# Graph attention on one Trainium2 core: degree rows, checks, strip loads and the last attention sums at other steps

## The chip, the core and the metric

The kernel runs on one core of a Trainium2 chip. The core has five engines that work side by side and wait for one another through semaphores: TensorE (PE in the profile, with its weight loads as PEld) multiplies matrices into PSUM, VectorE (DVE), ScalarE (ACT) and GpSimd (POOL) work elementwise, and SyncE (SP) issues transfers. The metric is the device time of one execution in microseconds.

## What is computed

A graph of N = 2708 nodes with D = 128 features, a 0/1 matrix `adj` of 2708 x 2708, in two layers. Only the first layer and its end matter here:

```python
def _L0_gnn_ref(t, x, adj, alpha, beta):
    deg = jnp.clip(adj.sum(axis=1), 1.0)
    dis = deg ** (-0.5)
    adj_norm = dis[:, None] * adj * dis[None, :]
    diffusion = adj_norm @ x - x
    norms = jnp.maximum(jnp.linalg.norm(x, axis=-1), COS_EPS)
    sim = x @ x.T / (norms[:, None] * norms[None, :])
    attn = jax.nn.softmax(beta * sim * adj, axis=1)
    return diffusion + jax.nn.sigmoid(alpha) * (attn @ x - x)

x = _layernorm(x + _L0_gnn_ref(L0_gnn_t, x, adj, L0_gnn_alpha, L0_gnn_beta), axis=-1)
x = _layernorm(x + _L1_gnn_ref(x, adj, L1_gnn_W, L1_gnn_a), axis=-1)
```

The second layer (`_L1_gnn_ref`: two products with `adj` around an attention without softmax) takes the time from about 300 us on and isn't touched.

## The kernel before

**Tiles.** The nodes are cut into NB = 22 blocks of 128 rows (the last holds 20) and into strips of SW = 512 columns: strips 0 to 4, and strip 5, the "side" strip, with the remaining 148 columns. Four blocks make a group, groups 0 to 5, the last of two blocks. `adj_t` is the transposed matrix; a "piece" is one group of blocks of one strip, 1024 KB.

**Attention.** The loop `for n, s in enumerate(order)` takes the strips in the order 2, 3, 4, 1, 0, so n = 0 is strip 2 ("the first place") and n = 4 is strip 0 (the last). The side strip is worked on together with n = 3. In each strip 22 steps k run over the blocks `jb` in the order `taken`: 8 to 21, then 4 to 7, then 0 to 3, that is over the groups 2, 3, 4, 5, 1, 0. A step does:

- TensorE makes `sim` (a product of the normalized rows, or, for blocks whose strip was done before, a transpose of a kept copy).
- VectorE multiplies it with beta and the piece into `p_t` (line 212; six buffers, EARLY + 3), ScalarE takes the exponential (line 217), GpSimd adds it to `total` (line 222), and TensorE adds `x_sb` times `p_t` to `att_acc` in PSUM (line 207). In the first strip, TensorE's last product lags three steps.
- When a group is through, its piece of the next strip is loaded into the same room on SP's queue.

Around these steps, work for later is put at fixed steps:

- `degree(ib, h)` loads half a row block of `adj` (677 KB, on SP) into one of three rooms, `row0`, `row1` and the back part of `x1` (blocks 6 and up; its front part is the `total` of n = 3), and ScalarE adds it up. There are 44 half rows; `rows_at[n]` lists the steps at which one is taken from the list `todo`.
- `roots(b0, b1)` turns the sums into `deg`, `live` and `dis` (the power -0.5, on GpSimd). `x_sb` is then scaled with `dis` on VectorE (line 742) after steps 11, 15, 19 and 21 of the last strip, block by block as the attention's products have read it.
- In the last strip, `round_part(g)` copies the pieces of strip 0 into tiles of the diffusion (VectorE, a cast), `check_part(g)` adds up the low 16 bits of a piece on ScalarE, writing its elementwise result into a scratch room, and `load_part(1, g)` loads the piece of strip 1 for the diffusion into the same room, issued on GpSimd's queue. A load needs the check, the rounding and all uses of the old piece.
- `attended(s, acc, total)` ends a strip: TensorE sums `total` over the partitions (`sums`, 8 small matmuls, line 528), VectorE takes reciprocals, ScalarE copies `acc` from PSUM (`to_sbuf`), TensorE turns it (`turned`), VectorE adds it to `att` (line 538). For a strip it stands at step 5 of the next one; for strip 0 it stands behind the loop.

**Diffusion.** After the loop `x_sb` is split into a rounded part and a rest, `x_hi` and `x_lo` (`halves`, line 224). Then `for s in (NS - 1, 0, 1, 2)` takes the strips 5, 0, 1, 2: `diffuse(s, acc)` adds up 22 blocks times two parts in `dif_acc` (the side strip uses `x_sb` itself, in one part), `load_strip(s + 2)` asks for the strip after next, and `summed_up`, `normed`, `x1_turned`, `scores`, `tally` and so on make the first layer's result out of it. `attended` of strip 0 stands behind the products of strip 5, before those of strip 0. Strips 3 and 4 follow in an order written out by hand.

**What sets the order.** Each engine works through its own list in order. `pinned` ties an instruction behind the last pinned one of its engine. In the first strip (`strict` holds an entry) all instructions of the helpers at lines 198 to 222 are pinned, in the order of the program. Later only what stands in `in_order(...)` is pinned, behind the step that it belongs to; all else is ordered by the builder, from its own estimate of when each instruction is ready, the earlier in the program first. Line 198 of the profile is the helper of pinned instructions, lines 207, 212, 217 and 222 those of unpinned ones on TensorE, VectorE, ScalarE and GpSimd.

PSUM: `ps_acc` has two banks for accumulators, `tp` and `tp2` are two banks handed out in turn by `tp_bank` for sums and transposes. SBUF: copies made by `to_sbuf` share two buffers.

Of the kernel before, what the change touches and what calls it, by code (L numbers as in the profile page):

```python
# [12 lines left out]
I16 = mybir.dt.int16  # L13
# [5 lines left out]
P = 128  # L19
N = 2708  # L20
D = 128
NB = (N + P - 1) // P
NP = NB * P
LAST = N - (NB - 1) * P
SW = 512
# [22 lines left out]
def grouped(  # L48
# [46 lines left out]
    x1 = late.tile([P, NB, D], F32, name="x1")  # L95
# [139 lines left out]
    def to_sbuf(acc, v, nb):  # L235

        t = lp.tile([P, SW], F32, tag="to_rows", name="tr_sb", bufs=2)
        if v < nb * P:
            nc.gpsimd.memset(t[:, v : nb * P], 0.0)
        act("copy", t[:, :v], acc[:, :v])  # L240
        return t
# [8 lines left out]
    def turned(t, nb):  # L250

        rows = tp_bank("tr_ps")
        for b in range(nb):
            mm(nc.tensor.transpose, rows[:, b, :], t[:, ts(b, P)], ident)
        return rows
# [38 lines left out]
    groups = list(dict.fromkeys(b // 4 for b in taken))  # L294
# [39 lines left out]
    with ExitStack() as es:  # L334
        pz = pool("pz", EARLY + 3, side="right", stack=es)
        pa = pool("pa", side="right", stack=es)
        row_rooms = [pa.tile([P, N // 2], F32, name=f"row{k}") for k in range(2)]
# [158 lines left out]
        def in_order(f):  # L496

            latest.update(behind)
            strict.append("some")
            f()  # L500
            strict.pop()
# [13 lines left out]
        def roots(b0, b1):  # L515

            t = deg[:, b0:b1]
            dve("tensor_tensor", t, deg2[:, b0:b1, 0], deg2[:, b0:b1, 1], ALU.add)
            dve("tensor_scalar", live[:, b0:b1], t, 0.0, None, ALU.is_gt)
            dve("tensor_scalar", t, t, 1.0, None, ALU.max)  # L520
            gps("tensor_tensor", dis[:, b0:b1], t, minus_half[:, b0:b1], ALU.pow)

        def attended(s, acc, total):

            v, nb = width(s), blocks(s)
            sums = tp_bank("sums")
            for b in range(nb):
                nc.tensor.matmul(
                    sums[:, b, 0:1], total[:, ts(b, P)], ones[:, 0:1], start=True, stop=True
                )  # L530
            rsum = small.tile([P, SW // P], F32, tag="rsum", name="rsum")
            nc.vector.reciprocal(rsum[:, :nb], sums[:, :nb, 0])
            nc.vector.tensor_scalar(rsum[:, :nb], rsum[:, :nb], sig, None, ALU.mult)
            rows = turned(to_sbuf(acc, v, nb), nb)
            for b in range(nb):
                ib = s * 4 + b
                r = att[:, ib, :]
                nc.vector.scalar_tensor_tensor(
                    r, rows[:, b, :], rsum[:, b : b + 1], r, ALU.mult, ALU.add
                )  # L540
# [1 line left out]

        room_of = {2: "room5", 3: "room1", 4: "room3", 1: "room0", 0: "room4", 5: "room2"}
        rounded_at = {2: 5, 3: 8, 4: 12, 1: 15, 0: 18, 5: 19}
        checked_at = {2: 13, 3: 18, 4: 21, 5: 21}
        strips = {0: {}, NS - 1: kept_c}

        def part_of(s, g):
# [10 lines left out]
        def check_part(g, room=None):  # L559
            low_bits_of(  # L560
                kept_a[g].rearrange("p b i -> p (b i)"),
                room or row_rooms[g % 2].bitcast(I16),
            )

        def load_part(s, g):
            src = adj_t[4 * g * P : min(4 * g + 4, NB) * P, ts(s, SW)]
            pinned(
                "strips", gps, "dma_start", part_of(s, g),
                src.rearrange("(b p) i -> p b i", p=P),
            )  # L570
# [6 lines left out]
        ended = []  # L577
        scaled = set()
        for n, s in enumerate(order):
            wide = n == side_n  # L580
            w_all = SW + SHORT if wide else SW
            acc = ps_acc.tile([P, SW], F32, tag="acc", name="att_acc")
            if wide:
                total = x1[:, :6, :].rearrange("p b i -> p (b i)")
# [3 lines left out]
            else:  # L588
                total = lp.tile([P, SW], F32, tag="total", name="total", bufs=2)
# [10 lines left out]
                (1, 17): lambda: constants(2),  # L600
                (2, 11): lambda: roots(0, 8),
                (3, 20): lambda: roots(8, 18),
                (4, 12): lambda: roots(18, NB),
            }

            rows_at = {
                0: (18, 20), 1: range(0, NB, 2), 2: range(0, NB, 2),
                3: [k for k in range(21) if k % 3 < 2], 4: range(0, 12, 2),
            }
            turns = {  # L610
                3: lambda: turn_rows(12, 16, by_dve),
# [20 lines left out]
            for k, jb in enumerate(taken):  # L632
# [91 lines left out]
                if n == len(order) - 1:  # L724
                    for g in [g for g, at in rounded_at.items() if at == k]:
                        in_order(lambda: round_part(g))
                    if k in (17, 20):
                        in_order(lambda: load_part(1, groups[k > 17]))
                    for g in [g for g, at in checked_at.items() if at == k]:
                        in_order(lambda: check_part(g))  # L730
                    if k in (11, 15, 19, 21):

                        done = sorted(taken[: k + 1 if k == NB - 1 else k - 1])
                        done = [b for b in done if b not in scaled]
                        scaled.update(done)
                        while done:
                            b0 = b1 = done[0]
                            while b1 in done:
                                done.remove(b1)
                                b1 += 1  # L740
                            xs = x_sb[:, b0:b1, :]
                            nc.vector.tensor_tensor(
                                xs, xs,
                                dis[:, b0:b1].unsqueeze(2).to_broadcast([P, b1 - b0, D]),
                                ALU.mult,
                            )
# [267 lines left out]
    for s in (NS - 1, 0, 1, 2):  # L1014
        acc = ps_acc.tile([P, SW], F32, tag="acc", name="dif_acc")
        diffuse(s, acc)
        if s < 3:
            load_strip(s + 2)
        if s == NS - 1:
            attended(*ended.pop())  # L1020
            for g in (1, 0):
                check_part(
                    g, work2.tile([P, 2048], I16, tag="low", name="low_junk", bufs=1)
                )
            for g in groups[2:]:
                load_part(1, g)
        if s == 1:
            flat = kept_c.rearrange("p b i -> p (b i)")
            v = SHORT
            for b0, b1 in ((0, NB // 2), (NB // 2, NB)):  # L1030
                low_bits_of(
                    flat[:, b0 * v : b1 * v],
                    work2.tile([P, 2048], I16, tag="low", name="low_junk", bufs=1),
                )
        normed(s, summed_up(s, acc))
        x1_t = x1_in_sbuf(s, x1_turned(s))
        pbs = []
        for k in (1, 0):
            pb = scores(s, x1_t, k, score_bank())
            tally(s, pb, k)  # L1040
            pbs.append(pb)
        shared_row(s, pbs[0])
        picked(s, pbs[0], sr_p)
        picked(s, pbs[1], sc_p)
        limited(s * 4, s * 4 + blocks(s))
        e2(s * 4, s * 4 + blocks(s))
        if s == 1:
            fill("e")
# [577 lines left out]
    k = 0  # L1626
# [568 lines left out]
```

## Time and profile before

| | |
|---|---|
| median of 3 runs | 649.35 us (648.65 to 652.32) |
| the profiled execution | 652.04 us, span 649.3 us |
| PE busy | 608.8 us, 94% |
| DVE busy | 491.4 us, 76% |
| ACT busy | 471.3 us, 73% |
| POOL busy | 289.2 us, 45% |
| first strip of the attention | about 9 to 50 us |
| last strip of the attention | about 174 to 219 us |
| diffusion | from 219.88 us (first product of strip 0) to about 290 us |

The span runs from the first to the last instruction of the profiled execution; its time has some 2.7 us more around it. That execution took 2.69 us more than the median of the runs. Sums of durations below come from this one execution.

Two engines share lines in the profile: where a tile's name ends in a digit the digit is left out, so `x<-` can be `x1`, and `row<-pieces` is a check that writes its scratch into `row0` or `row1`.

### The profile page before, as it was taken

Reading aid. Unit: us, or ns where it says so; the run is one execution under the profiler, and the core shown is the slowest. Engines: PE = TensorE matmul, PEld = TensorE weight load, DVE = VectorE, ACT = ScalarE, POOL = GpSimd, SP = SyncE. Lnnn points to the kernel's source line nnn. Section 1 sums busy time; section 2 is a strip of 40 time slices with the busy share of each in tenths; the row PEclk is TensorE's granted clock in tenths of the full one; section 3 lists DMA queues with packets and bytes.
Section 4 is the critical chain, followed back from the end, with each engine's and each line's share of the span. In section 5 each row is a group of like instructions: output and inputs, shape, how many; then the busy total and the mean of one; then the engine's idle time right before and its main releaser. Section 6 shows DMA issues by size and latency. Waiting matters only on the chain.

```text
span 649.3 us, 8555 instructions
## 1 busy us (share of the span) xinstructions
PE 608.8 (94%) x2859; PEld 351.9 (54%) x2859; DVE 491.4 (76%) x978; ACT 471.3 (73%) x649; POOL 289.2 (45%) x270
## 2 busy tenths in 40 slices
PE   7999999999999899998878899999999999989993
PEld 4445345465655676765664344444444444658872
DVE  5765865764699756756885999899999999599575
ACT  4767786767889521410585999999999999778652
POOL 6967778777798742000123322333232230021573
PEclk9999999999999899999988999999999999999997
DMA  8968989988971999989956999756689453259981
GB/s 270 392 221 330 317 301 363 360 329 310 335 262 70 276 390 389 387 267 375 394 205 185 238 223 246 214 168 175 193 217 267 170 170 129 87 202 383 390 320 53
DMA packets 66407, 171.64 MB, mean 264 GB/s; under 512 B 10059, under 2 KB 19285, under 8 KB 63333
## 3 DMA queue, kind: packets, MB, share of 16 engines
q1 hardware_dynamic: 42500, 107.01, 46.4%
q0 software_dynamic: 22464, 62.25, 34.5%
q10 hardware_dynamic: 1392, 1.77, 0.8%
q8 instruction: 24, 0.39, 0.2%
q14 instruction: 27, 0.21, 0.1%
HBM read 171.89 MB, written 5.72 MB: 274 GB/s over the span
## 4 chain that ended last, share of the span: by engine, by line
PE 65%; ACT 13%; DVE 10%; POOL 6%; issue 4%; DMA 1%; another core or an unknown queue 0%; DVEq 0%; POOLq 0%; ACTq 0%
PE num L198 11%; PE m_acc L198 11%; PE att_acc L207 9%; PE h_acc L1690 7%; PE sim L207 7%; PE dif_acc L207 6%; ACT q L198 5%; POOL total L222 4%; ACT L198 2%; DVE q L198 2%; PE tot L198 2%; PE dif_acc L198 1%; PE sim L198 1%; POOL ss L198 1%; ACT xn L198 1%
## 5 line engine op out<-in xcount | busy, mean ns | idle before, releaser
L198 PE MATMUL m_acc<-q,xws 128*128 128x512 f32 x240 | 121.6, 592 | 0.0
L198 PE MATMUL num<-ring,wt 128*128 128x512 f32 x216 | 98.2, 546 | 3.6 <-DVE q L198 2.2
L222 POOL TENSOR_TENSOR total<-total,p_t 128x512 f32<-128x512 f32 (+1 forms) x67 | 91.8, 1370 | 21.0 <-ACT p_t L217 18.4
L207 PE MATMUL att_acc<-p_t,x_sb 128*128 128x512 f32 x184 | 91.1, 602 | 1.1 <-ACT p_t L217 1.1
L212 DVE SCALAR_TENSOR_TENSOR p_t<-sim,gentle,pieces 128x512 f32<-128x512 f32 x89 | 65.0, 746 | 34.8 <-PE sim L207 25.7
L198 DVE SCALAR_TENSOR_TENSOR q<-sr_b,nc_s,q 128x1536 f32<-128x1536 f32 (+1 forms) x48 | 77.8, 1623 | 17.3 <-ACT q L198 17.3
L217 ACT ACTIVATE p_t<-p_t,shift 128x512 f32<-128x512 f32 (+1 forms) x89 | 64.7, 745 | 33.8 <-DVE p_t L212 31.5
L198 DVE COPY q<-num 128x512 f32<-128x512 f32 (+1 forms) x142 | 83.5, 611 | 4.5 <-PE num L198 4.5
L198 PEld LDWEIGHTS m_acc<-q,xws 128*128 128x128 f32 x240 | 45.3, 190 | 55.0 <-issue 54.8
L198 ACT ACTIVATE q<-q,head,rest 128x1536 f32<-128x1536 f32 (+1 forms) x48 | 70.2, 1508 | 1.6 <-DVE ring L198 1.3
L198 ACT ACT_TABLE_LOAD x52 | 66.7, 1283 | 3.9 <-issue 3.1
L198 PEld LDWEIGHTS num<-ring,wt 128*128 128x128 f32 x216 | 39.0, 190 | 49.1 <-issue 34.2
L198 ACT ACTIVATE q<-q,c_s 128x1536 f32<-128x1536 f32 (+1 forms) x48 | 62.9, 1355 | 0.3
L198 POOL DMA_INDIRECT ring<-in_adj_t,k_no x18 | 20.8, 1154 | 89.1 <-PE num L198 85.6
L207 PEld LDWEIGHTS att_acc<-p_t,x_sb 128*128 128x128 f32 x184 | 31.7, 189 | 35.3 <-ACT p_t L217 18.8
L207 PE MATMUL sim<-xn_t 128*128 128x512 f32 x98 | 47.6, 592 | 0.0
L222 POOL TENSOR_TENSOR x<-x,p_t 128x660 f32<-128x660 f32 (+1 forms) x22 | 35.1, 1596 | 11.3 <-ACT p_t L217 10.6
L198 ACT ACTIVATE row<-row 128x1354 f32<-128x1354 f32 x30 | 39.5, 1318 | 0.3 <-DMA row<-in_adj 0.3
L207 PE MATMUL dif_acc<-strip,x_hi 128*128 128x512 f32 x88 | 37.8, 429 | 0.0
L207 PE MATMUL dif_acc<-strip,x_lo 128*128 128x512 f32 x88 | 36.2, 411 | 0.0
L1690 PE MATMUL h_acc<-rounded,m_hi 128*128 128x512 f32 x88 | 32.4, 407 | 3.7 <-DVE rounded L212 3.7
L198 PE MATMUL num<-x_sb,wt 128*128 128x512 f32 (+1 forms) x72 | 34.4, 570 | 0.7 <-ACT gb L198 0.7
(362 smaller groups left out, 1170.6 us busy)
## 6 DMA issues: line engine op xcount, KB each, us to landing
pieces<-in_adj_t SPq DMA_DIRECT2D x24, 1024.0 KB, 6.8
strip<-in_adj_t POOLq DMA_DIRECT2D x20, 1024.0 KB, 18.3
row<-in_adj SPq DMA_DIRECT2D x30, 677.0 KB, 5.5
nat<-in_adj_t SPq DMA_DIRECT2D x19, 768.0 KB, 7.7
x<-in_adj SPq DMA_DIRECT2D x14, 677.0 KB, 6.2
ring<-in_adj_t SPq DMA_DIRECT2D x9, 1024.0 KB, 5.1
pieces<-in_adj_t SPq DMA_DIRECT2D x7, 512.0 KB, 6.4
x_sb<-in_adj_t SPq DMA_DIRECT2D x4, 768.0 KB, 6.2
```

What stands on the lines that cost most here:

```text
L198: latest[engine] = op(*args, **kwargs)
L207: op(*args, **kwargs)
L212: return getattr(nc.vector, op)(*args, **kwargs)
L217: return getattr(nc.scalar, op)(*args, **kwargs)
L222: return getattr(nc.gpsimd, op)(*args, **kwargs)
L1690: nc.tensor.matmul(acc[:, : rows.shape[-1]], m[:, kb, :], rows, start=(kb, part) == (0, 0), stop=(kb, part) == (NB - 1, 1),)
```

## The change

- `rows_at`: the first strip takes half rows at steps 13, 15, 17, 18 and 20 instead of 18 and 20; the last one at steps 0, 2 and 4 instead of 0, 2, 4, 6, 8 and 10. All half rows in between keep their steps, and each step now takes the row that is three places further in the list.
- `prep`: the last roots stand at step 7 of the last strip instead of 12.
- `checked_at`: checks of groups 2, 3, 4, 5 stand at steps 9, 13, 18, 20 instead of 13, 18, 21, 21, and their scratch room is the back part of `x1` instead of `row0` and `row1`.
- `asked_at`: the loads of strip 1's groups 2 and 3 stand at steps 13 and 16 instead of 17 and 20.
- `attended` of strip 0 is split: the copy out of PSUM (`to_sbuf`) stays behind strip 5's products, and the rest (sums, transposes, VectorE's part) stands behind strip 0's products.

```diff
--- before.py
+++ after.py
@@ -520,7 +520,7 @@
             dve("tensor_scalar", t, t, 1.0, None, ALU.max)
             gps("tensor_tensor", dis[:, b0:b1], t, minus_half[:, b0:b1], ALU.pow)
 
-        def attended(s, acc, total):
+        def attended(s, acc, total, t=None):
 
             v, nb = width(s), blocks(s)
             sums = tp_bank("sums")
@@ -531,7 +531,7 @@
             rsum = small.tile([P, SW // P], F32, tag="rsum", name="rsum")
             nc.vector.reciprocal(rsum[:, :nb], sums[:, :nb, 0])
             nc.vector.tensor_scalar(rsum[:, :nb], rsum[:, :nb], sig, None, ALU.mult)
-            rows = turned(to_sbuf(acc, v, nb), nb)
+            rows = turned(t or to_sbuf(acc, v, nb), nb)
             for b in range(nb):
                 ib = s * 4 + b
                 r = att[:, ib, :]
@@ -542,7 +542,8 @@
 
         room_of = {2: "room5", 3: "room1", 4: "room3", 1: "room0", 0: "room4", 5: "room2"}
         rounded_at = {2: 5, 3: 8, 4: 12, 1: 15, 0: 18, 5: 19}
-        checked_at = {2: 13, 3: 18, 4: 21, 5: 21}
+        checked_at = {2: 9, 3: 13, 4: 18, 5: 20}
+        asked_at = {2: 13, 3: 16}
         strips = {0: {}, NS - 1: kept_c}
 
         def part_of(s, g):
@@ -559,7 +560,7 @@
         def check_part(g, room=None):
             low_bits_of(
                 kept_a[g].rearrange("p b i -> p (b i)"),
-                room or row_rooms[g % 2].bitcast(I16),
+                room or x1[:, 6:, :].rearrange("p b i -> p (b i)").bitcast(I16),
             )
 
         def load_part(s, g):
@@ -600,12 +601,12 @@
                 (1, 17): lambda: constants(2),
                 (2, 11): lambda: roots(0, 8),
                 (3, 20): lambda: roots(8, 18),
-                (4, 12): lambda: roots(18, NB),
+                (4, 7): lambda: roots(18, NB),
             }
 
             rows_at = {
-                0: (18, 20), 1: range(0, NB, 2), 2: range(0, NB, 2),
-                3: [k for k in range(21) if k % 3 < 2], 4: range(0, 12, 2),
+                0: (13, 15, 17, 18, 20), 1: range(0, NB, 2), 2: range(0, NB, 2),
+                3: [k for k in range(21) if k % 3 < 2], 4: (0, 2, 4),
             }
             turns = {
                 3: lambda: turn_rows(12, 16, by_dve),
@@ -724,8 +725,8 @@
                 if n == len(order) - 1:
                     for g in [g for g, at in rounded_at.items() if at == k]:
                         in_order(lambda: round_part(g))
-                    if k in (17, 20):
-                        in_order(lambda: load_part(1, groups[k > 17]))
+                    for g in [g for g, at in asked_at.items() if at == k]:
+                        in_order(lambda: load_part(1, g))
                     for g in [g for g, at in checked_at.items() if at == k]:
                         in_order(lambda: check_part(g))
                     if k in (11, 15, 19, 21):
@@ -1017,13 +1018,15 @@
         if s < 3:
             load_strip(s + 2)
         if s == NS - 1:
-            attended(*ended.pop())
+            in_sbuf = to_sbuf(ended[0][1], SW, SW // P)
             for g in (1, 0):
                 check_part(
                     g, work2.tile([P, 2048], I16, tag="low", name="low_junk", bufs=1)
                 )
             for g in groups[2:]:
                 load_part(1, g)
+        if s == 0:
+            attended(*ended.pop(), in_sbuf)
         if s == 1:
             flat = kept_c.rearrange("p b i -> p (b i)")
             v = SHORT
```

## The prediction

> **What bounds the kernel now.** I read the share of busy time first, then the stretches around the change, then the chain of waits, then each engine in order of time. TensorE is busy 94% of the span, so a change pays only where TensorE stands still, and that is the end of the attention:
>
> ```profile
> 187.00:206.00 19.00, 18.86 (x69) 10.08 (x69) 18.86 (x23) 18.66 (x27) 17.84 (x10) 1.00 0.47 153
> ```
> ```profile
> 206.00:220.00 14.00, 10.14 (x54) 7.25 (x52) 11.10 (x12) 10.14 (x15) 12.59 (x13) 0.98 0.42 115
> ```
>
> The columns are stretch, length, then busy time of PE, PEld, DVE, ACT, POOL, granted clock, DMA share and GB/s. From 187 to 206 four engines are full at once. From 206 to 220 TensorE is idle for 14.00 - 10.14 = 3.86 us: this is what there is to win here. GpSimd is the fullest there. The chain of waits says the same:
>
> ```profile
> 205.55 1.53 issue
> 207.19 0.92 issue
> 208.11 1.27 POOL total L222
> ...
> 217.28 1.29 POOL total L222
> 218.62 1.08 PE sums L528 x8
> ```
>
> The chain runs along GpSimd's additions, stops 1.5 us in front of the roots, and ends in the sums of strip 0. The order of time shows why it stopped (VectorE, then TensorE):
>
> ```profile
> 204.34 1.23 DVE L198 TENSOR_TENSOR deg<-deg 128x4 f32<-128x4 f32 x1
> 205.49 0.74 DVE L212 SCALAR_TENSOR_TENSOR p_t<-sim,gentle,pieces 128x512 f32<-128x512 f32 x1
> 206.15 0.15 DVE L198 TENSOR_SCALAR live<-deg 128x4 f32<-128x4 f32 x1
> 206.22 0.74 DVE L212 SCALAR_TENSOR_TENSOR p_t<-sim,gentle,pieces 128x512 f32<-128x512 f32 x1
> 206.88 0.15 DVE L198 TENSOR_SCALAR deg<-deg 128x4 f32<-128x4 f32 x1
> 208.17 3.43 DVE L742 TENSOR_TENSOR x_sb<-x_sb,dis 128x512 f32<-128x512 f32 x2 [1.14 <-POOL dis L198]
> 213.37 0.69 DVE L742 TENSOR_TENSOR x_sb<-x_sb,dis 128x512 f32<-128x512 f32 x1 [1.76 <-PE att_acc L207]
> 213.97 1.43 DVE L212 CAST x_hi<-x_sb 128x384 fp32r<-128x384 f32 x1
> ```
> ```profile
> 209.98 0.77 PE L207 MATMUL dif_acc<-side,x_sb 128*128 128x148 f32 x4 [1.31 <-DVE x_sb L742]
> 210.59 2.74 PE L207 MATMUL att_acc<-p_t,x_sb 128*128 128x512 f32 x6
> ...
> 218.62 1.08 PE L528 MATMUL sums<-ones,total 128*128 128x1 f32 x8 [2.55 <-POOL total L222]
> ```
>
> One late number goes round all engines. The last half row is added up behind step 10 (ScalarE, done at 200.97). Its degrees reach VectorE at 204.34, the root is ready on GpSimd at 208.13, the scaling of x_sb waits 1.14 for it, TensorE waits 1.31 for the scaling, and the last att_acc products queue behind that. The last scaling waits 1.76 for them, and only then does x_hi start, without which no product of strip 0's diffusion can. Last, TensorE waits 2.55 for the sums.
>
> **The change, part by part.** The yardstick is the first dif_acc product of strip 0, at 219.88 now; from there to 270 TensorE shows no idle time, so a shift there is handed on.
>
> Rows. A half row costs ScalarE 1.31 us (199.66 to 200.97). Three go from the last strip to steps 13, 15 and 17 of the first, 3.9 us each way. In the first strip ScalarE waited 1.43, 1.43 and 0.98 us before the exponentials that follow those steps, so two are covered and the third makes one exponential 0.33 us late; TensorE's products lag three steps there (3 x 1.72 us), which hides that. Their transfers (3 x 677 KB, 2.08 MB) are issued on SP in front of pieces of the next strip, which are not used before 50 us; 40 to 50 moved 178 GB/s against 391 at 20 to 30, so there is room. Cost taken: 0; without the cover 3.9 us (see the slower rival).
>
> Roots at step 7. The deg, live, max, dis and scaling instructions are the same, only earlier. The waits 1.14 and 1.76 shrink, and 0.72 us in front of the ten-wide deg at 177.51 goes too, since the half row it waited for is three places earlier. All three would be 3.6 us of VectorE. VectorE was gapless from 187 to 206, and the two scalings that took 3.43 us now fall among the last p_t, so the 1.76 can't go wholly: the last p_t is pushed later by what is pulled forward. I take 0.72 + 1.14 + 1.0 = 2.9 us earlier for x_hi; bounds 0.7 (only the first wait) and 3.6.
>
> Checks at steps 9, 13, 18, 20. A full check costs 1.89 us (200.97 to 202.86), the half one 1.05. In front of the last exponential stand now 6 rows and 2 checks, 7.9 + 3.8 = 11.7 us; after it 3 rows, 3 checks and the half one, 3.9 + 5.7 + 1.1 = 10.7. ScalarE gains 1.0 us, which VectorE, as full, doesn't let through: 0 taken, and up to 1.0 lost if the checks stand in front of a late p_t. Their scratch room moves to x1's back part, which the last half row but two leaves at step 0: no wait.
>
> Loads of strip 1 at 13 and 16. Their two issues on GpSimd (0.98 and 0.79 us, at 211.00 and 216.47) come in front of additions that release p_t buffers. Six buffers: p_t 21 needs addition 15, done 205.54, and began at 206.22, so 0.68 us of slack. dis (1.02) and one issue (0.98) now come before it, 2.0 us, against 0.96 us of GpSimd waiting at 186 that may vanish. VectorE may so lose 0.4 us, inside the 0.76 kept back above. What waits behind an issue that waits for its check: all later additions; check 2 is 4 steps ahead, check 3 is 3 ahead, as near as now, so 0. The two transfers (2.1 MB) then run at 200 to 210, where DMA moves 0 GB/s now, and leave the full stretch from 219 (386 to 397 GB/s) with 2.1 MB less, 5.4 us: diffusion that starts 3 to 5 us earlier still finds its strips.
>
> GpSimd itself loses the 1.57 us wait for deg: its last addition ends about 217.0 instead of 218.56.
>
> Sums of strip 0 behind its products. The PSUM copy stays where it was; 8 sums matmuls, 4 transposes, and reciprocal, product and 4 additions on VectorE (0.17 + 0.22 + 1.13) go behind the products. The x_lo part for the first blocks ended at 216.80 + 2.19 = 218.99, so of the sums' 2.55 us wait only 219.88 - 218.99 = 0.9 was theirs alone; the rest is VectorE's. What they cost TensorE (218.62 to 219.88, less overlap, 1.1) is paid later. The normalization of strip 0 starts 1.5 us of VectorE later; the 10 us of strip 1's products cover that, and without them it costs 1.5. The next PSUM bank is free for the side strip's transposes at once, which stood at 224.35 and 232.70; VectorE's 8.55 us wait after 224.4 is filled by that.
>
> Clock. After the 2.55 us gap the granted clock was 0.50 from 219.25 to 222.9, and 8 products took about 0.42 us apart instead of 0.23: 1.6 us. With x_hi 2.9 us earlier the gap in front of strip 0 is some 2 to 2.5 us: I take half, 0.8, bounds 0 and 1.6. The Trainium skill ("TensorE: Matmul & The Clock Gate", § What's actually happening) has the clock fall after an idle window of about 3.4 us that runs freely. The row shows that a 2.55 us gap inside one sufficed. By the page as it stands a shorter gap would bring the whole 1.6; by the row, with luck, none.
>
> Against the change speaks the skill's "GPSIMD Engine Reference" (§ Key points): GpSimd shares its SBUF interfaces with VectorE's two-input or two-port instructions. The trace agrees: an addition takes 1.27 us alone and 2.14 to 2.41 beside a cast or a scaling. This is why the pulled-forward scalings are not free.
>
> Sum: -2.9 (x_hi) - 0.9 (sums off the path) + 1.1 (sums paid later) - 0.8 (clock) = **-3.5 us**. The profiled execution took 652.04 us (span 649.3), which becomes 648.5; it lies above the median of 649.35, on which the same shift gives **645.9**. Bounds: -0.7 - 0.9 + 1.1 + 1.0 (checks) = +0.5 on one side; -3.6 - 0.9 + 1.1 - 1.6 - 1.5 (deeper reordering, up to the 3.86 us idle plus the clock's 1.6 in all) = -6.5 on the other.
>
> **Rivals.**
> (a) GpSimd still sets the end. It is busy 12.59 of 14 us, and x_hi's 384 columns took 1.43 us beside it where 768 later took 0.55. If x_lo isn't ready before GpSimd's end at 217 and its own 0.7 to 1.2 us behind it, products start at 218.2: -1.7 + 1.1 = -0.6, 648.7. Against it: the first casts finished while additions still ran.
> (b) The change doesn't do what it says: nothing pins the sums, and the builder orders them by its own costs; left in front, they hold TensorE until GpSimd's end, 1.6 us earlier than now: 647.8. The present trace speaks for it, since the sums were placed before products that were nearly ready.
> (c) Slower: a half row lands late in the first strip, where every ScalarE instruction is in a fixed order. The fourth and fifth rows need rooms that the first two leave at about 37 and 41 us, and SP is in order: it waits up to 7.5 us for p_t before a piece. If row five stands behind the piece issued at 49.58 now, it lands 5.5 us later, at 55.1, instead of 48.5: ScalarE stands for 6.6 us, and beyond the cover of 5.2 us all engines do. It decides once a row is over 5.2 us late; with the cover used up by the fourth row (behind the issue at 42.71, 3.5 us late) the price is 6.6, so +6.6 - 3.5 = +3.1: 652.5. Against it: ScalarE waits for rows 0.3 us in the whole trace now.
>
> **How the numbers follow.** Under 0.5% (3.25 us) can't be told from no change here. Forecast 0.55: its own range is 642.8 to 648, and four fifths of it lie below 646.1. (a) 0.15, (b) 0.10, (c) 0.20. Faster 0.44, same 0.11 + 0.25 = 0.36, slower 0.20. The range 642.8 to 651.0 leaves out the worst half of (c) and a little at the fast end.
>
> **What would show it.** Right: in the last strip no wait of dis for deg nor of x_sb for dis; x_hi starting about 211 and the first product of strip 0 about 216, with sums near 227; nothing lost at 35 to 50. Half right: clock 0.50 in front of strip 0 again. Wrong: GpSimd's last addition still about 218 with x_lo behind it; sums in front of the products; a wait of ScalarE for a row before 50 us; TensorE waiting for strips at 230 to 280, which would hand the gain back.

## The result, and the profile after

The change made the kernel slower. Median 653.91 us after (651.55 to 662.68, 18 runs) against 650.42 us before (648.65 to 653.25, 18 runs): ratio 1.0054, 95% interval 1.0040 to 1.0069. The slowest of the 18 runs after (662.68) was in a slower state of the chip, at a granted clock of 0.973, and is left out of the ratio. The forecast was 645.9, at most 651.0.

The profiled execution of after took 657.65 us (span 655.9), 3.7 above its own median, so its differences are sorted into lasting and chance before they are used. From the order of time of the two traces, in us:

| stretch | before | after | difference |
|---|---|---|---|
| start to the side strip's sums (end of the fourth strip) | 185.47 | 187.08 | +1.61 |
| to strip 0's first product (the yardstick) | 34.41 | 34.81 | +0.40 |
| to the last dif_acc product | 68.88 | 68.55 | -0.33 |
| to the first num product | 56.86 | 59.20 | +2.34 |
| to the last num product | 211.36 | 212.20 | +0.84 |
| to the issue of the last output | 87.56 | 87.48 | -0.08 |
| to the end of the span | 4.80 | 6.54 | +1.74 |
| time outside the span | 2.69 | 1.79 | -0.90 |

The two rows that end at num products are not tied to the change: roots_12 below, which differs from after by one step number, needs 56.43 us in the first, and the second is 208.9 to 209.2 us in 13 of the 20 profiles of this study and 210.5 to 212.2 in seven, before among them. The first row's 1.61 us lies in the third strip (38.71 us from sums to sums, 37.45 before) and, with 0.41 us, in the second; the fourth takes 0.67 us more and the side strip's sums come 0.75 us less behind it. The 0.41 us were chance: copies_moved below, which is the same program up to there, needs 39.80 us in the second strip, as before. What lasts is so 1.2 us in the third strip, nothing gained in the last strip, and 1.74 - 0.90 = 0.8 us at the end, of which it will stay open whether it costs time. The medians differ by 3.5, so about 1.5 us has no place in the table. The forecast of 3.5 us was to come out of the second and third rows.

The stretches around the change, same columns as before (stretch, length, busy time of PE, PEld, DVE, ACT, POOL, granted clock, DMA share, GB/s):

```profile
187.00:206.00 19.00, 17.44 (x71) 9.82 (x70) 18.82 (x25) 16.36 (x24) 16.18 (x11) 1.00 0.18 69
206.00:220.00 14.00, 9.86 (x38) 5.47 (x37) 12.96 (x11) 6.82 (x10) 12.42 (x12) 1.00 0.91 260
```

ScalarE lost 18.66 - 16.36 = 2.3 us of work in the first and 10.14 - 6.82 = 3.3 in the second; of these 5.6 us the three half rows are 3.9. VectorE is as full as it was in the first, and has 12.96 where it had 11.10 in the second. TensorE is idle 4.14 us in the second, not 3.86. The chain of waits has changed engines (start, us, what; the scaling of `x_sb`, line 742 before, is line 743 here and line 746 where a cast is moved below):

```profile
205.21 3.21 DVE strip L198
208.42 0.91 DVE x_sb L743
...
210.75 1.01 DVE strip L198
211.76 1.90 DVE x_sb L743
...
213.84 0.75 DVE p_t L212
...
214.62 0.73 ACT p_t L217
...
215.39 1.12 PE att_acc L207 x2
...
218.17 5.83 PE dif_acc L207 x38
```

No GpSimd addition is left in it. It runs along VectorE: a cast of strip 0 and a scaling, a second cast and a second scaling, and only then the last p_t, its exponential, its att_acc products. TensorE's order of time shows what waits:

```profile
211.62 1.13 PE L207 MATMUL att_acc<-p_t,x_sb 128*128 128x512 f32 x2 [2.35 <-ACT p_t L217]
...
215.39 1.12 PE L207 MATMUL att_acc<-p_t,x_sb 128*128 128x512 f32 x2 [1.79 <-ACT p_t L217]
216.35 0.92 PE L207 MATMUL dif_acc<-side,x_sb 128*128 128x148 f32 x6
217.11 1.06 PE L207 MATMUL att_acc<-p_t,x_sb 128*128 128x512 f32 x2
218.01 4.15 PE L207 MATMUL dif_acc<-side,x_sb 128*128 128x148 f32 x30
221.89 0.49 PE L207 MATMUL dif_acc<-strip,x_hi 128*128 128x512 f32 x1
```

The last att_acc products, over at 213.33 before (210.59 + 2.74), end at 218.17, and most of the side strip's products stand behind them. The roots are early, as meant: the 1.14 and 1.76 us waits of the scalings are gone. But p_t 21 starts at 214.50 instead of 206.22. TensorE has no gap from 215.39 to the first product of strip 0 at 221.89, so x_hi, at 215.16, is not what that product waits for.

In the third strip VectorE's first roots (128x8) now stand in a row. Before, then after:

```profile
108.98 0.20 DVE L198 TENSOR_TENSOR deg<-deg 128x8 f32<-128x8 f32 x1
109.10 0.74 DVE L212 SCALAR_TENSOR_TENSOR p_t<-sim,gentle,pieces 128x512 f32<-128x512 f32 x1
109.77 0.15 DVE L198 TENSOR_SCALAR live<-deg 128x8 f32<-128x8 f32 x1
109.95 0.17 DVE L198 TENSOR_SCALAR deg<-deg 128x8 f32<-128x8 f32 x1
```
```profile
108.55 1.06 DVE L198 TENSOR_TENSOR deg<-deg 128x8 f32<-128x8 f32 x1
109.64 0.17 DVE L198 TENSOR_SCALAR live<-deg 128x8 f32<-128x8 f32 x1
109.85 1.11 DVE L198 TENSOR_SCALAR deg<-deg 128x8 f32<-128x8 f32 x1
```

Three more half rows in the first strip mean that every later step takes a half row three places further on, so what hangs on them is ready earlier and is put elsewhere. Two instructions of eight columns took 1.06 and 1.11 us; ScalarE then waited 2.26 us for p_t and TensorE 1.58 us at 112.42.

### The profile page after: what moved, and what is told of

It is laid out like the page before. It is cut to its first block, busy times and chain, and to the rows that moved or that the text cites. A ratio compares the mean times of both kernels' runs of the same rounds, so it can differ in the third digit from the quotient of the medians.

```text
span 655.9 us, 8555 instructions
## 1 busy us (share of the span) xinstructions
PE 609.5 (93%) x2859; PEld 352.1 (54%) x2859; DVE 496.9 (76%) x978; ACT 474.0 (72%) x651; POOL 289.3 (44%) x270
## 4 chain that ended last, share of the span: by engine, by line
PE 71%; DVE 10%; ACT 6%; DMA 5%; issue 4%; POOL 2%; DVEq 0%; ACTq 0%; POOLq 0%
PE num L198 14%; PE m_acc L198 14%; PE att_acc L207 9%; PE h_acc L1693 7%; PE dif_acc L207 7%; PE sim L207 7%; DMA wt<-g_d 3%; PE tot L198 2%; DVE p_t L212 1%; DMA x<-in_adj 1%; ACT q L198 1%; PE dif_acc L198 1%; PE sb_ps L207 1%; PE sim L198 1%; DVE onp L198 1%
## 5 line engine op out<-in xcount | busy, mean ns | idle before, releaser
L207 PE MATMUL dif_acc<-strip,x_hi 128*128 128x512 f32 x88 | 36.2, 411 | 0.0
L198 PE MATMUL num<-x_sb,wt 128*128 128x512 f32 (+1 forms) x72 | 33.0, 549 | 1.2 <-ACT gb L198 0.7
```

What stands on the lines that cost most here:

```text
L198: latest[engine] = op(*args, **kwargs)
L207: op(*args, **kwargs)
```

## The experiments

**One part alone.** Where an expectation counts strips by their sums, it is in their order in the attention. Each kernel here applies one part of the change to before, its hunks as shown with the change.

only_sums: the hunks of attended, in_sbuf and `if s == 0:`.

> The kernel before, with one part of the change: the sums of strip 0 behind its products; rows, roots, checks and loads as before. VectorE's order of the last strip is then that of before. Theory 1 (the moved half rows reorder VectorE and TensorE in the last strip, and this costs the 3.5 us): between 1.5 us faster and 0.5 us slower than before, first product of strip 0 about 219. Theory 2 (the late sums push strip 0's normalization and cost it): 1.5 to 3 us slower. Theory 3 (the first strip or the strips after it are disturbed by the rows): as theory 1.

only_rows:

```diff
-                0: (18, 20), 1: range(0, NB, 2), 2: range(0, NB, 2),
-                3: [k for k in range(21) if k % 3 < 2], 4: range(0, 12, 2),
+                0: (13, 15, 17, 18, 20), 1: range(0, NB, 2), 2: range(0, NB, 2),
+                3: [k for k in range(21) if k % 3 < 2], 4: (0, 2, 4),
```

> The kernel before, with the half rows of the change alone (first strip 13, 15, 17, 18, 20, last strip 0, 2, 4); roots at step 12, checks, loads and sums as before. Theory 1: 2 to 4 us slower than before, the last att_acc product 3 us or more after 212.7, p_t of steps 20 and 21 behind two scalings. Theory 2: within 0.5 us of before. Theory 3: 1.5 to 3 us slower, all of it there before the last strip begins (sums of the third strip's end over 1.5 us later than 178.4).

only_checks: checked_at, asked_at and the room in x1.

> The kernel before, with the checks and the loads of strip 1 alone at their new steps and with the new scratch room; rows, roots and sums as before. Theory 1: -0.5 to +1.5 us, since the order changes less here. Theory 2 and 3: within 0.5 us. A fourth theory (the two load issues in front of GpSimd's additions hold p_t's buffers): 1.5 to 3 us slower.

Measured: only_sums 651.27 us, ratio 1.0010 (0.9993 to 1.0027); only_rows 651.13, 1.0012 (0.9995 to 1.0029); only_checks 651.37, 1.0021 (1.0005 to 1.0038). No part alone is the culprit. The three together (0.43%) come near the whole (0.54%), but two of the three can't be told from nothing. The roots at step 7 were not run alone. The sums alone bring the first product to 215.84, 4 us earlier, for nothing:

```profile
215.84 0.49 PE L207 MATMUL dif_acc<-strip,x_hi 128*128 128x512 f32 x1
219.30 0.67 PE L207 MATMUL dif_acc<-strip,x_lo 128*128 128x512 f32 x1 [2.98 <-DVE x_lo L212]
```

TensorE waits 2.98 us for VectorE's x_lo (219.3 there, 218.99 before), falls to clock 0.50 at 219.5, and reaches strip 1's products only 0.6 us earlier (230.90 against 231.54). The rows alone lose 1.9 us between the first strip's sums and the fourth's (122.29 against 120.36), none before (58.05 against 58.00), and gain as much behind them up to the last dif_acc product (108.46 against 110.40). The checks alone move the scalings among the last p_t as well; TensorE waits 3.07 us at 207.72 for one, the clock is 0.50 for 3.4 us from 207.4 on, and the first product is at 221.65. So late sums are not the cause, the strips between are part of it, and a reordering of the last strip shows in all that move work into it.

**One part changed in after.**

scale_behind:

```diff
-                    if k in (11, 15, 19, 21):
+                    if k in (11, 21):
...
-                            nc.vector.tensor_tensor(
-                                xs, xs,
+                            in_order(lambda: dve(
+                                "tensor_tensor", xs, xs,
```

> The changed kernel, with the scalings of x_sb that stood after steps 15 and 19 put behind the last p_t, in a fixed order. Theory 1, in its narrow form (the scalings in front of the last p_t are what costs): 2 us or more faster than the changed kernel, about 651.5. Theory 1 in its wide form (TensorE's order, in which most of the side strip's products stand behind the last att_acc): under 1 us of gain. Theory 2 and 3: no gain, 653.5 to 654.

654.83 us, 1.0088 (1.0057 to 1.0118): slower still. The last p_t came 2.4 us earlier (212.12) and the last att_acc products with it, but:

```profile
214.65 1.93 PE L207 MATMUL dif_acc<-side,x_sb 128*128 128x148 f32 x14
221.63 3.91 PE L207 MATMUL dif_acc<-side,x_sb 128*128 128x148 f32 x16 [5.06 <-DVE x_sb L198]
225.28 0.49 PE L207 MATMUL dif_acc<-strip,x_hi 128*128 128x512 f32 x1
```

The scalings cost more late than early: VectorE did both casts x_hi (3.96 us) and an x_lo (1.60 us) in front of the last of them, and the clock was 0.50 for 3.4 us from 221.6 on. So it isn't the scalings' place alone.

first_roots_14 (the first roots three steps later), old_checks (checked_at, the loads' steps and the room as before), roots_12, old_sums (attended as before):

```diff
-                (2, 11): lambda: roots(0, 8),
+                (2, 14): lambda: roots(0, 8),
```

> The changed kernel with the first roots (blocks 0 to 7) at step 14 of the third strip instead of 11; nothing else. Theory A (the earlier rows let the three VectorE operations of these roots stand in a row, where they meet GpSimd's additions twice, 1.06 and 1.11 us instead of 0.20 and 0.17, and TensorE stands 1.58 us): the 1.3 us that the third strip lost come back, the end of the third strip 1.0 to 1.5 us earlier than in the changed kernel, the time about 652.6. Theory B (the loss lies behind the diffusion, in the stretch from its last product to the second layer, 2.3 us longer in the changed kernel's trace): the time within 0.7 us of the changed kernel.

> The changed kernel with checks, loads and scratch room as before; rows, roots and sums as changed. If the moved checks and loads cost (theory C: their issues on GpSimd and the checks on ScalarE stand in front of the last additions and exponentials): 1 to 2.5 us faster than the changed kernel, about 652. If rows and sums alone explain the loss: within 0.7 us of 653.9.

```diff
-                (4, 7): lambda: roots(18, NB),
+                (4, 12): lambda: roots(18, NB),
```

> The changed kernel with the last roots at step 12 again. The order on VectorE hardly changes by this, so all theories of the last strip expect the time of the changed kernel, 653.9 within 0.7 us; the trace is a second look at the stretch behind the diffusion: theory B expects it about 2 us longer than before again (59 us from the last product of the diffusion to the first num product, against 57), otherwise it was chance.

> The changed kernel with the sums of strip 0 in front of its products again; rows, roots, checks and loads as changed. If the late sums are no loss (they took 4 us from the wait in front of strip 0's first product when made alone, and gave them back to VectorE's late x_lo): 0.5 to 1.5 us slower than the changed kernel. If they are a loss: 0.5 to 1.5 us faster, about 653.

653.90 us, 1.0047 (1.0018 to 1.0077); 655.47, 1.0084 (1.0054 to 1.0114); 654.88, 1.0061 (1.0033 to 1.0089); 654.25, 1.0056 (1.0032 to 1.0079). Undoing one part gives nothing back. first_roots_14 still needed 122.47 us from the first strip's sums to the fourth's (after 122.71), so the first roots' step is not the cause there by itself; its third strip took 38.05 us (after 38.71, before 37.45), its second, which comes ahead of the moved roots, 40.64 (40.21, 39.80), which is chance. From the side strip's sums to the first product roots_12 needs 34.81 us, exactly after's time: with the half rows done early, VectorE's roots stand at the same place with either step. old_checks needs 33.09, but TensorE then waits 3.48 us at 280.9.

**The strips between, and the end of the program.** The end shows a pattern in the trace's records of ScalarE's sequencer: where ScalarE has more than 768 instructions (its waits and table loads among them), the 769th starts 1.65 to 2.35 us after the one before it (in after 652.87 and 654.93). The change adds four: two waits and two table loads, since the square roots and exponentials of the diffusion change places once more. Two kernels take up each question.

middle_as_before (three of the last half rows first, the first roots in two steps):

```diff
         todo = [(ib, h) for ib in range(NB) for h in range(2)]
+        todo = todo[41:] + todo[:41]
...
-                (2, 11): lambda: roots(0, 8),
+                (2, 11): lambda: added(0, 8),
+                (2, 12): lambda: roots(0, 8, False),
```

> After, with the three extra half rows of the first place being the last three in the matrix (so the strips between take the same half rows at the same steps as before) and the first roots' addition at step 11, their other two VectorE instructions at step 12 of the third strip. VectorE's order in the strips between is then as before. Theory M (the order of the roots in the strips between costs about 2 us): from the sums of strip 1 to those of strip 4 120.4 us instead of 122.7 (before 120.4), and 653.9 - 2.2 = 651.7 us, ratio about 1.002. Rival (the lost time comes from the rows' transfers or from the first strip and not from this order): 122.5 again and 653.9 us, ratio 1.005.

652.95 us, 1.0030 (1.0010 to 1.0051). From the first strip's sums to the fourth's it took 121.75, not half of the way to the 120.4 expected; the third strip is mended (37.36 us, before 37.45, after 38.71), and 0.8 us of what is missing lie in its second strip (40.60 us; rows_best below, with the same edit, 39.85). At the side strip's sums nothing of it is left, 187.07 against 187.08, for now the ten-wide roots are dearer, 3.34 us in three instructions against 2.78 in before and 0.50 in after:

```profile
180.03 1.21 DVE L198 TENSOR_TENSOR deg<-deg 128x10 f32<-128x10 f32 x1
...
181.56 1.35 DVE L198 TENSOR_SCALAR live<-deg 128x10 f32<-128x10 f32 x1
```

and TensorE waits 0.90 us at 184.25. So the loss can be pushed from one strip to the next. Theory M is right on the place, not on the 2 us: rows_best needs 121.01 us where only_rows needs 122.29, so 1.3 us of only_rows' 1.9 come back, and at its side strip's sums they are gone too (128.53 us from the first strip's sums, only_rows 128.65).

one_copy_more:

```diff
+    idle = const.tile([P, 1], F32, name="idle")
+    for _ in range(1):
+        nc.scalar.copy(idle, eps)
```

> Before, plus one copy of one element per partition on ScalarE while it loads at the start; with its wait ScalarE has 770 instructions instead of 768. Theory F (ScalarE's instruction 769 waits for a fetch of code, which comes at the very end of the program): from the landing of the last output to the end of the span 3.6 to 4.0 us instead of 1.8, and 1.0 to 2.0 us more in all, 651.4 to 652.4 us, ratio 1.0015 to 1.003, with nothing else moved. Rival (the longer tail of the other runs has another cause): 1.8 us again and 650.4 us.

copies_moved:

```diff
-            nc.scalar.copy(mine[:, :w_], acc[:, :w_])
+            (nc.scalar.copy if final else nc.vector.tensor_copy)(mine[:, :w_], acc[:, :w_])
```

> After, with four of the five copies of h_acc (not the last one) on VectorE instead of ScalarE: ScalarE has 766 instructions instead of 772. Theory F: from the landing of the last output to the end of the span 1.8 us instead of 3.6, the last strips of h_acc within 0.5 us of after, and 653.9 - 1.0 to 2.0 = 651.9 to 652.9 us, ratio 1.0025 to 1.004. Rival: the tail stays at 3.6 us and the time at 653.9 us, ratio 1.005.

rows_best (only_rows with both edits):

> Before with the half rows moved and nothing else of the change (roots of the last strip at step 12, old checks, loads and sums), the strips between kept as before by the order of half rows and roots of the first run, and the four copies of h_acc on VectorE: ScalarE has 766 instructions. If M and F both hold, the half rows' own gain of 1.9 us in the last strip is all that is left: 650.4 - 1.9 = 648.5 us, ratio 0.997. With M alone 649.5, with F alone 650.0, with neither 651.1 us, ratio 1.001.

649.98 us, 0.9992 (0.9969 to 1.0015); 651.74, 1.0026 (1.0002 to 1.0050); 649.39, 0.9981 (0.9960 to 1.0001). From the traces:

```
kernel              ScalarE       last output's issue   outside    both
                    instructions  to end of span, us    the span   together
before_cast_copies  763           5.09                  2.07       7.16
copies_moved        766           5.21                  1.87       7.07
only_sums           767           5.02                  2.69       7.71
before              768           4.80                  2.69       7.50
before_cast_moved   769           5.64                  1.60       7.24
one_copy_more       770           6.04                  1.95       7.99
only_checks         771           6.16                  1.85       8.01
after               772           6.54                  1.79       8.33
only_rows           772           6.76                  1.97       8.73
```

One more copy (and a table load with it) lengthens the span's end by 1.2 us, and four copies fewer shorten after's by 1.3. But the time outside the span differs too, and together 0.5 and 1.3 us remain, too little for these intervals: one_copy_more was no slower, and rows_best, expected at 0.997, can't be told from 0.999. The time outside the span is no chance of one execution: over all runs it is 2.5 to 2.7 us in the mean for before, 1.7 to 2.0 for each kernel with a 769th instruction, and 2.0 to 2.4 for the others. So spans alone overstate what the late instruction costs. Why it is late was not shown.

**Who fills the last strip?** Theory V says VectorE's own time, theory G GpSimd's additions. A cast of strip 0 goes to ScalarE, after_cast_moved in after, before_cast_moved in before:

```diff
         def round_part(g):
-            dve("tensor_copy", part_of(0, g), kept_a[g])
+            if g in (0,):
+                act("copy", part_of(0, g), kept_a[g])
+            else:
+                dve("tensor_copy", part_of(0, g), kept_a[g])
```

> After, with the cast of step 18 (128x2048, 3.21 us on VectorE at 205.21 beside GpSimd's additions) on ScalarE, which waits 2.91 and 3.05 us for p_t just there. Theory V (VectorE's own time is what fills the last strip, so that work pulled forward on it only pushes the last p_t back): p_t 20 at about 211 instead of 213.84, the first dif_acc product of strip 0 at about 219.5 instead of 221.89, and 653.9 - 2.4 = 651.5 us, ratio 1.002. Theory G (GpSimd's additions set it, whatever VectorE does): its last addition at 221.5 to 222 and the first product within 0.5 us of 221.9; 653.9 us, ratio 1.005.

> Before, with the same cast on ScalarE (1.22 us on VectorE there, behind which the chain of roots and scalings stands). V: that chain 0.6 to 1.2 us earlier, first product at 218.7 to 219.3 instead of 219.88, ratio 0.998 to 0.999. G or the late last half row (ScalarE done with it at 200.97, later with the cast in front): 219.9 or later, ratio 1.000 to 1.002.

650.66 us, 1.0009 (0.9995 to 1.0023), and 646.95 us, 0.9943 (0.9921 to 0.9964). In after_cast_moved, ScalarE, VectorE, then TensorE:

```profile
205.71 1.88 ACT L198 CAST strip<-pieces 128x2048 fp32r<-128x2048 f32 x1
```
```profile
204.96 2.68 DVE L746 TENSOR_TENSOR x_sb<-x_sb,dis 128x512 f32<-128x512 f32 x1
...
210.94 1.40 DVE L212 SCALAR_TENSOR_TENSOR p_t<-sim,gentle,pieces 128x512 f32<-128x512 f32 x2
```
```profile
218.65 1.27 PE L207 MATMUL dif_acc<-side,x_sb 128*128 128x148 f32 x8 [1.12 <-DVE x_sb L746]
219.66 0.49 PE L207 MATMUL dif_acc<-strip,x_hi 128*128 128x512 f32 x1
```

p_t 20 is at 210.94 (expected 211), the first product at 219.66 (expected 219.5). GpSimd's last addition, its work unchanged, ended at 219.72 instead of 221.95: it follows. V holds, G falls. One instruction gave back 0.45% of the 0.54% that the change had lost. In before_cast_moved VectorE shows the chain of roots and scalings of the old order, and what remained to wait for (the cast that was moved took 1.67 us at 201.06 in before, not the 1.22 us that the expectation has):

```profile
204.93 0.75 DVE L212 SCALAR_TENSOR_TENSOR p_t<-sim,gentle,pieces 128x512 f32<-128x512 f32 x1
206.16 1.76 DVE L746 TENSOR_TENSOR x_sb<-x_sb,dis 128x512 f32<-128x512 f32 x1 [0.47 <-POOL dis L198]
207.84 0.74 DVE L212 SCALAR_TENSOR_TENSOR p_t<-sim,gentle,pieces 128x512 f32<-128x512 f32 x1
208.50 1.09 DVE L746 TENSOR_TENSOR x_sb<-x_sb,dis 128x512 f32<-128x512 f32 x1
213.54 0.99 DVE L746 TENSOR_TENSOR x_sb<-x_sb,dis 128x512 f32<-128x512 f32 x1 [3.94 <-PE att_acc L207]
```

The first product is at 217.26, 2.6 us earlier (0.6 to 1.2 expected). The longest gap before it is 1.08 us, not 2.55, and the half clock in front of strip 0 is gone; the last dif_acc product is 4.1 us earlier (284.64 against 288.76). More than VectorE's own 1.67 us came back, and part of it is GpSimd's: 15 of its additions, the first at 188 us, took 23.71 us instead of 25.09, and the sums start as the last of them ends, at 216.01. In after_cast_moved the 16 additions took 24.51 us instead of 24.94. So VectorE's time is what fills the last strip, but how much of the gain is VectorE's own work and how much comes from the two engines slowing each other less, these runs don't separate.

after_three_mended (after with middle_as_before, copies_moved and the cast) and rows_best_casts (rows_best with `g in (0, 1)`):

> After with three losses taken out: half rows and first roots between the first and the last strip as in middle_as_before, four copies of h_acc on VectorE as in copies_moved (766 instructions on ScalarE), and the cast of step 18 on ScalarE. If V holds beside the two others: 653.9 - 1.0 - 0.8 - 2.4 = 649.7 us, ratio 0.999; if V falls 652.1, ratio 1.0025. First product at 219.5 against 221.9.

> rows_best with the casts of steps 15 and 18 on ScalarE. V: of rows_best's waits of ScalarE for p_t in the last strip (2.23, 1.60, 2.25 us) most go, first product 1.5 to 2.5 us earlier than 220.92, and 649.4 - 2 = 647.4 us, ratio 0.995. G: first product within 0.5 us of 220.9, 649.4 us, ratio 0.998.

649.20 us, 0.9986 (0.9970 to 1.0003), as V would have it; 647.67, 0.9968 (0.9945 to 0.9992), where V expected 0.995 and G 0.998, so the time doesn't decide here. The trace does: the first product is 3.1 us earlier than in rows_best (217.81 against 220.92), more than expected.

before_cast_copies (before_cast_moved with the copies) and before_two_casts (the same with `g in (0, 5)`):

> before_cast_moved with the four copies of h_acc on VectorE: 763 instructions on ScalarE instead of 769. Theory F: end of the last output's issue to end of span 4.8 to 5.2 us instead of 5.64, and 646.95 - 0.5 = 646.4 us, ratio 0.9935. Rival (the end of the program costs nothing in time): 646.9, ratio 0.9943. First product of strip 0 at 217.3 in both.

> before_cast_copies with the cast of step 19 (128x1024, 1.20 us at 202.26 in front of the roots) on ScalarE too. V: VectorE's roots and scalings 1 us earlier; but ScalarE then has 1 us more in front of its last p_t, and GpSimd's last addition was already at 216.0, so 0 to 1 us: first product 216.3 to 217.3, 645.4 to 646.4 us, ratio 0.992 to 0.9935.

647.12 us, 0.9932 (0.9910 to 0.9954), and 645.54 us, 0.9920 (0.9899 to 0.9941). The first can't be told from before_cast_moved, so what the end of the program costs in time stays open. The second has the lowest median of the study and beats before and after; from the two kernels with one cast it can't be told. Its two stretches:

```profile
187.00:206.00 19.00, 18.86 (x69) 10.04 (x69) 17.78 (x23) 18.66 (x27) 18.19 (x12) 1.00 0.46 149
206.00:220.00 14.00, 13.21 (x69) 9.65 (x68) 9.66 (x15) 13.26 (x18) 11.89 (x14) 1.00 0.73 212
```

VectorE has 9.66 us of work in the second where it had 11.10, and TensorE is busy 13.21 instead of 10.14. The half rows stay where they were.

## Why the prediction was wrong

**The step that failed** is "Roots at step 7", with "I take 0.72 + 1.14 + 1.0 = 2.9 us earlier for x_hi". The rows of after behind it (VectorE):

```profile
199.17 2.30 DVE L198 CAST strip<-pieces 128x2048 fp32r<-128x2048 f32 x1
...
205.21 3.21 DVE L198 CAST strip<-pieces 128x2048 fp32r<-128x2048 f32 x1
208.34 1.75 DVE L743 TENSOR_TENSOR x_sb<-x_sb,dis 128x512 f32<-128x512 f32 x1
...
211.69 2.23 DVE L743 TENSOR_TENSOR x_sb<-x_sb,dis 128x512 f32<-128x512 f32 x1
213.84 1.40 DVE L212 SCALAR_TENSOR_TENSOR p_t<-sim,gentle,pieces 128x512 f32<-128x512 f32 x2
215.16 0.82 DVE L212 CAST x_hi<-x_sb 128x384 fp32r<-128x384 f32 x2
```

x_hi started at 215.16 instead of 213.97; counted from the side strip's sums, so without the loss ahead of it, 0.42 us earlier, below even the lower bound of 0.7. Nor did x_hi set the first product any more, which came 6.7 us behind it: the last p_t did, through the att_acc and side strip products queued on TensorE. The text saw that the last p_t is pushed later by what is pulled forward, and kept back 0.76 us for it; p_t 21 came 8.28 us later, 6.67 counted from the side strip's sums. Its own first row said why: VectorE had 18.86 of 19 us. As long as an engine has no idle time, an earlier input moves nothing earlier on it; it only changes the order. And the new order was dearer: between 187 and 222 the four casts of 2048 columns took 1.99 us in the mean against 1.45 (185 to 220 before), the three scalings of 512 columns 1.91 against 1.40, in all 3.7 us more, against 2.1 us less for the first two x_hi. The reading "One late number goes round all engines" was half of the chain; the other half, that the casts shared VectorE with it, was in the same rows and was not priced. after_cast_moved and before_cast_moved show it. Of the signs that the text gave, the waits of dis for deg and of x_sb for dis did vanish; x_hi was to start about 211 and the first product of strip 0 about 216, and came at 215.16 and 221.89.

**Rows, "Cost taken: 0"**: right where it was argued, in the first strip (its sums at 58.02 against 58.00), and so rival (c) fell: no half row was late. Wrong by 1.2 us (only_rows, up to the side strip's sums) in the third strip, which the step did not look at: the list of half rows is one list, and three more at its head move every later one. This term, put at nothing, is the largest part of the loss that has a place.

**Sums, -0.9 and +1.1**: the first is right, the second somewhat small. In only_sums, counted from the side strip's sums, strip 1's products came 0.9 us earlier and the last dif_acc product 0.8 us later, so 1.7 us were paid. The sums did move (to 233.85 in after, where 227 was expected), so rival (b) fell, and alone they changed nothing that can be told, for x_lo was not ready either.

**Checks and loads, 0 with up to 1.0 lost**: only_checks lost 0.21% (1.4 us), which is a little more. Its trace places 0.4 us of this between the side strip's sums and the last dif_acc product, and 0.5 us at the end of the program; the rest has no place. The transfers were about as forecast: DMA share 0.91 from 206 to 220, and TensorE waits for no strip afterwards.

**Clock, -0.8**: the half clock before strip 0 did go (before 219.5 to 222.9, where the text has 219.25; after has none before 299), and this is luck in part: after has gaps of 2.35 and 1.79 us there, and in copies_moved, where the first of them is 2.34 us, the clock was 0.50 for 3.4 us from 212.8 on. In the table it is part of the -0.33 us from the first product on, beside the sums paid there.

**The range**: its fast end goes by -6.5 us, past the limit that the text sets beside it, 3.86 + 1.6 = 5.5 us. The miss is at the other end, so this decided nothing.

**Rival (a)**, GpSimd still sets the end: its last addition did end late, at 221.95, but as a follower. "Slower" had a chance of 0.20, given to a mechanism that did not happen.

## What to carry to other kernels

Where the profile shows an engine without idle time in a stretch, ask what an earlier input can move there: here it moved 0.42 us of 2.9. Taking one instruction off that engine and giving it to one that waits in the same stretch gave 0.45% in after and 0.57% in before. When the head of a shared list of work is changed, look at everything that hangs on its later entries. The Trainium skill ("Perfetto Trace Analysis", § Optimizing Scalar/DVE Operations) advises to move work to ScalarE when VectorE is saturated and warns of GpSimd's shared port; the runs agree, with 0.57% for one cast and 0.80% for two casts and four copies.

## What was not expected of the hardware

- A cast of 128x2048 took VectorE 1.22 us at 188.12 in before; the two of steps 15 and 18 took 1.68 and 1.67 us in before, and 2.30 and 3.21 us in after, beside GpSimd's additions. On ScalarE such a cast took 1.88 to 1.89 us in all six kernels that had one there. VectorE's roots, of four to ten columns, took 0.15 to 0.20 us or 0.58 to 1.36 us. The Trainium skill ("Trainium Architecture — The Big Picture", § What this means for kernel authors) calls the port pair that VectorE and GpSimd share an exclusive lock; these durations, either short or 0.4 to 2 us longer, agree with that (the cast of 3.21 us ended 1.09 us behind the end of the 1.28 us addition that began 0.84 us after its start), though no run took the additions away.
- A gap of TensorE of 2.55 us (before), 2.98 us (only_sums) or 2.34 us (copies_moved) came with 3.4 us at clock 0.50; gaps of 2.35 and 1.79 us (after) or 1.08 us (before_cast_moved) did not. So the length of the gap does not decide alone.
- ScalarE's 769th instruction started 1.65 to 2.35 us after the one before it in each of the twelve kernels that have one, here always at the very end of the program.
